# Attention inside a scan-paced kernel: one stream of 64 steps with the values product two steps behind the scores, and the branch announced earlier

## The chip, the cores and the metric

The kernel runs on one core of one Trainium2 chip. The metric is the time of one execution on the device, in microseconds (us); the time before is the median of three runs. Engines are called PE (TensorE, the matrix engine; PEld is its weight load), DVE (VectorE), ACT (ScalarE), POOL (GpSimd) and SP (SyncE, which issues nearly all DMAs). Each engine takes its instructions from a queue of its own, in the order in which the program was built.

## The reference, cut to what matters

Four images of 1024 tokens with 256 channels go through a layer with a convolution and a state-space scan (64 states), a grouped convolution, graph attention with a mixture of experts, and a second state-space layer (16 states) with another mixture of experts. The part that the change touches is the attention over 4096 tokens with 8 heads of 32 channels and a mask from an edge list:

```python
Q, K, V = (proj(Wq, bq), proj(Wk, bk), proj(Wv, bv))
scores = jnp.einsum('bhnd,bhmd->bhnm', Q, K) / jnp.sqrt(jnp.float32(hd))
mask = jnp.zeros((N, N), dtype=bool).at[edge_index[0], edge_index[1]].set(True)
scores = jnp.where(mask[None, None], scores, -jnp.inf)
attn = jax.nn.softmax(scores, axis=-1)
attended = jnp.einsum('bhnm,bhmd->bhnd', attn, V)
...
out = attended @ Wo + bo
y = x + out
```

A layer norm of `y` follows. The x that enters holds 4 images of 1024 tokens, each of which the kernel handles as a batch of its own with the same mask, so there are four attentions of 1024 x 1024 x 8.

## The kernel before, in words

**The scan sets the frame.** `scans` (L364) walks 1280 units. For unit k, SP loads `dA` (512 KB, replicated, `load`, four units ahead), ACT takes its exponential (`decay`, two units ahead), PE spreads the input into a two-bank PSUM tile `ps_rep` (`first`, one unit ahead, two buffers), DVE multiplies it by a row (1.2 us) and runs the scan (2.3 us), POOL multiplies the result by another row, and every second unit PE collects two results into `ps_y` (`pair`). The order of each engine's queue is written out by this loop.

**The stages ride along.** Everything else is a list of stages (`STAGES`), written as generators. Twice per unit the loop may run pieces of the current stage up to its next `yield` (`advance`, L538), at most `TICKS` = 2 pieces at a time and only while a table of assumed costs (`Metered.COST`) says that no engine is ahead of DVE's clock. The values that are yielded aren't used for that. So a `yield` is a place where scan instructions can slip in between. When a scan needs the output of a stage that isn't done, the rest of that stage is built with no scan beside it (`need`, L525; the flag `self.alone`). That happens in the fourth attention, from its 25th step of 64 on.

**Attention** (`attention`, L1174) projects queries, keys and values, bounds the scores (`large_scores`), adds two bias rows on POOL, and then calls `shift` (L1299) and `all_heads` (L1234).

- `shift`: where the bound is too large for a plain exponential, row maxima are computed and put into `mT`; with the given inputs the flag `large` is 0 and the work is skipped. Four engines (PE, DVE, ACT, SP) load the flag into a register and take a `tc.Switch` with two arms there and then. POOL takes no part.
- `heads` (L1377) handles one pair of heads against one half of the queries in eight steps, one per block of 128 keys. `scores(kb)` runs two f32 products of depth 32 into two PSUM tiles `ps_sc` (tag "s", two buffers in all), adds `mT` and the mask as bf16 products, and ACT writes the exponentials of both heads to `p` (three buffers). `values(kb)` multiplies `p` by the values and by ones (for the row sums), four f32 products into four column groups of the PSUM tile `acc` (one buffer). With a scan beside it the order is `pipe(scores, values, cut=True)`: values one step behind scores, and a `yield` after each. Alone, an empty step is put between them, so values are two steps behind, and the scores use the larger PSUM tiles of the scan (`ps_sx`) with one exponential of 128x1024.
- After eight steps the pipe runs empty, and ACT copies `acc` to `raw` and `sums`. After every second pair `divided` follows (a reciprocal on DVE, a product on POOL), interleaved with the next pair's steps.
- `projected` (L1435) multiplies half of the attended tokens by `Wo` into PSUM tiles that `ps` hands out in turn (tags "s", "s", "acc"); DVE adds. For the first half of the queries it stands between two head pairs of the second half, and `normed` is interleaved with the pair after that.

```python
        if alone:
            yield from self.pipe(range(TB), scores, lambda kb: None, values, cost=1.3)
        else:
            yield from self.pipe(range(TB), scores, values, cost=1.3, cut=True)
        nc.scalar.copy(raw[at : at + 64, c, :], acc[:64, :])
        nc.scalar.copy(sums[at : at + 64, c, :], acc[64:, :])
```

Of the kernel before, what the change touches and what calls it, by code (L numbers as in the profile page):

```python
# [7 lines left out]
F32 = mybir.dt.float32  # L8
# [8 lines left out]
P = 128  # L17
NB = 4
L = 1024
TB = L // P  # L20
C = 256
# [111 lines left out]
class Hybrid:  # L133
    def __init__(self, ctx, tc, a, out):
        self.ctx, self.tc, self.nc, self.a = ctx, tc, tc.nc, a
        self.out = out.rearrange("b h w c -> (b h w) c")
        nc = self.nc
        self.const = const = ctx.enter_context(tc.tile_pool(name="const", bufs=1))
        self.dram = ctx.enter_context(tc.tile_pool(name="dram", bufs=1, space=DRAM))

        self.ident = const.tile([P, P], F32, name="ident")
        make_identity(nc, self.ident)
        self.identb = const.tile([P, P], BF16, name="identb")
        nc.vector.tensor_copy(self.identb, self.ident)
# [12 lines left out]
        self.w_in0 = self.weight(const, "L0_conv_w_in", 2)  # L157
        for _ in self.norm(const, self.x0, TB, self.x0, "ln0"):
            pass

        self.blocks = const.tile([P, P], F32, name="blocks")
        make_block_diagonal(nc, self.blocks, 4)
        self.states = {0: 64, 3: 16}
        self.mem = {}


# [1007 lines left out]
    def attention(self, b, tb):  # L1174
        nc, tc, vec = self.nc, self.tc, self.vec
        with tc.tile_pool(name=f"at{b}", bufs=1, side="right") as op:
            xa = op.tile([P, TB, C], F32, name="xa")
# [8 lines left out]
            with tc.tile_pool(name=f"aa{b}", bufs=1, side="right") as fp:  # L1186
# [5 lines left out]
                def project(item):  # L1192
# [16 lines left out]
                    project, cost=1.7,  # L1209
# [14 lines left out]
                    nc.scalar.copy(v[:, 2 * j : 2 * j + 2, :], ps)  # L1224

                yield from self.pipe(range(TB // 2), values, cost=1.7)
            yield from self.add_rows(xa, self.bo, TB)
            yield from self.add_rows(tb, self.beta, TB)
            with tc.tile_pool(name=f"ab{b}", bufs=1, side="right") as fp:
                yield from self.shift(fp, qT, kT, mT, maskT, large)  # L1230
            with tc.tile_pool(name=f"ac{b}", bufs=1, side="right") as fp:
                yield from self.all_heads(fp, tb, qT, kT, v, maskT, mT, xa, wo)

    def all_heads(self, fp, tb, qT, kT, v, maskT, mT, xa, wo):  # L1234
        nc = self.nc

        def divided(raw, sums, c):
            nc.vector.reciprocal(sums[:, c, :], sums[:, c, :])
            yield 2.0
            nc.gpsimd.tensor_tensor(raw[:, c, :], raw[:, c, :], sums[:, c, :], ALU.mult)  # L1240
            yield 0.5

        then = iter(())
        for nh in range(2):
            raw, sums = (fp.tile([P, 2, 512], F32, tag=t, name=t, bufs=2) for t in ("raw", "sums"))
            for hp in range(4):
                for n, cost in enumerate(self.heads(fp, raw, sums, qT, kT, v, maskT, mT, nh, hp)):
# [12 lines left out]
            first = raw  # L1262
        yield from then
        y = yield from self.projected(fp, 1, raw, xa, wo)
        yield from self.normed(fp, tb, 1, y)

    def large_scores(self, fp, qT, kT, large):

# [27 lines left out]
        nc.vector.tensor_copy(large, most[:, 0:1])  # L1296
        yield 0.5

    def shift(self, fp, qT, kT, mT, maskT, large):  # L1299


        nc, tc = self.nc, self.tc
        E = mybir.EngineType
        go = {
            E.PE: nc.tensor, E.DVE: nc.vector, E.Activation: nc.scalar, E.SP: nc.sync,
        }
# [67 lines left out]

        yield from self.pipe([(c, g) for c in range(2) for g in range(2)], turn, cost=0.8)

    def heads(self, fp, raw, sums, qT, kT, v, maskT, mT, nh, hp):  # L1377

        nc = self.nc
        qs = slice(nh * 512, (nh + 1) * 512)
        c, at = hp // 2, 64 * (hp % 2)
        alone = self.alone
        acc = self.psum.tile([P, 512], F32, tag="acc", name="ps_at", bufs=1)
        got = {}

        def scores(kb):
# [11 lines left out]
            for i in range(2):  # L1401
# [4 lines left out]
            got[kb] = p = fp.tile([P, 2, 512], F32, tag="p", name="p", bufs=3)  # L1406
# [7 lines left out]
            for i in range(2):  # L1414
                nc.scalar.activation(p[:, i, :], two[i], AF.Exp)

        def values(kb):
            p = got.pop(kb)
            for i in range(4):
                h = 2 * hp + i % 2  # L1420
                nc.tensor.matmul(
                    acc[32 * i : 32 * i + 32, :],
                    lhsT=v[:, kb, h * HD : (h + 1) * HD] if i < 2 else self.ones,
                    rhs=p[:, i % 2, :],
                    start=(kb == 0), stop=(kb == TB - 1), tile_position=(0, 32 * i),
                )
# [490 lines left out]
```

## Time and profile before

| | |
|---|---|
| median of 3 runs | 6605.04 us (6598.39 to 6610.3) |
| the profiled execution: its time | 6610.56 us |
| the profiled execution: span, first to last instruction | 6608.8 us |
| mean granted PE clock | 0.834 |
| scan units | 1280: multiply 1213 ns, scan 2284 ns on DVE |
| attentions, first to last scores (us from the span's start) | 1420.7 to 1696.5, 2541.2 to 2817.4, 3954.0 to 4231.7, 5363.4 to 5584.6 |
| last scan-free stretch of attention 3 | from 5464.3 |
| an exponential, `p` | 595 ns (128x512), 1023 ns (128x1024) |
| a copy of `acc` (ACT) | 577 and 581 ns |
| `sums` reciprocal (DVE), `raw` product (POOL) | 3327 and 1266 ns |
| `y_at` add of a projection (DVE) | 692 ns |
| loads of the flag `large` on the sequencers of PE, DVE, ACT, SP | about 0.3 us each, at 1409.8 to 1413.5 in attention 0 |
| end of the write of `large` by DVE, attention 0 | 1388.9 |

All instructions that the planner counts are recorded in one helper, so nearly all have line L124 in the profile; they are told apart by the tiles that they write. "x<-y" means that tile x is written from y; an f32 product shows as two records. The name behind an idle time is what ended the wait; "issue" means that the engine waited for nothing that the profile shows. A busy PE isn't a PE at its peak, since the ends of its matmuls are modelled; the distance from one start to the next is the surer measure.

### The profile page before, as it was taken

What the parts mean: (1) busy time and instruction counts of PE and PEld (TensorE: products, weight loads), DVE (VectorE), ACT (ScalarE), POOL (GpSimd) and SP (SyncE); (2) the same over time, 40 slices, a digit from 0 to 9 for tenths busy, and PEclk for the clock granted to TensorE, in tenths of its full rate; (3) what the DMA queues carried; (4) which work ended last, traced back from release to release, by engine and by line L of the source; (5) the groups of instructions that cost most, each with busy time, mean ns of one, the idle gap of its engine ahead of it and who ended that gap; (6) DMA issues with size and microseconds to landing.
All of it is one profiled execution on the core that took longest, in us unless ns stands there. A gap on an engine that the chain in (4) does not pass through costs nothing. (4 is left out here: it accounts for less than half of the span.)

```text
span 6608.8 us, 59799 instructions
## 1 busy us (share of the span) xinstructions
PE 5331.1 (81%) x20236; PEld 2161.6 (33%) x20320; DVE 5140.0 (78%) x4310; ACT 3438.2 (52%) x4113; POOL 3642.9 (55%) x1793
## 2 busy tenths in 40 slices
PE   6667868679797568979689779898699688978979
PEld 2022312222342022234145232243255222524656
DVE  3978989988799997889889987898999971248411
ACT  3346566345477334557558445477487344245411
POOL 2857677755458665545856665556756651055200
PEclk8667868689798579979789789898699789877989
DMA  2454555643355566335645664345555750156221
GB/s 103 145 161 159 175 165 163 192 141 113 109 167 173 183 169 152 112 119 179 190 143 170 196 157 129 107 143 174 185 164 163 198 135 15 45 144 159 72 64 35
DMA packets 348113, 936.91 MB, mean 142 GB/s; under 512 B 37140, under 2 KB 119648, under 8 KB 346144
## 3 DMA queue, kind: packets, MB, share of 16 engines
q1 hardware_dynamic: 345616, 930.35, 46.3%
q0 software_dynamic: 2128, 2.13, 0.2%
q8 instruction: 172, 2.82, 0.2%
q14 instruction: 197, 1.61, 0.1%
HBM read 842.59 MB, written 93.95 MB: 142 GB/s over the span
## 5 line engine op out<-in xcount | busy, mean ns | idle before, releaser
L124 POOL TENSOR_TENSOR h<-h,rows 128x1024 f32<-128x1024 f32 x1280 | 3029.7, 2369 | 1948.9 <-DVE h L124 1736.3
L124 DVE TENSOR_TENSOR_SCAN h<-dA,ps_rep 128x1024 f32<-128x1024 f32 x1280 | 2923.9, 2284 | 169.3 <-issue 31.2
L124 DVE TENSOR_TENSOR ps_rep<-ps_rep,rows 128x1024 f32<-128x1024 f32 x1280 | 1552.8, 1213 | 254.0 <-PE ps_rep L124 253.7
L124 ACT ACTIVATE dA<-dA,A_L_conv_A_log 128x1024 f32<-128x1024 f32 x1024 | 1149.8, 1145 | 598.6 <-DMA dA<-dt 554.5
L124 PE MATMUL ps_rep<-S,spread_L_conv_A_log 96*128 96x512 bf16 x2048 | 762.1, 462 | 715.3 <-DVE h L124 694.5
L124 PE MATMUL ps_y<-h,collect_L_conv_A_log 128*32 128x512 f32 x4096 | 795.5, 759 | 70.4 <-POOL h L124 69.9
L124 PE MATMUL ps_h<-xTm,we 128*128 128x512 f32 x1536 | 717.2, 606 | 1.4 <-DVE tb L124 1.4
L124 PE MATMUL ps_e<-we,h_m 128*128 128x256 f32 x3072 | 699.3, 380 | 2.3 <-ACT h_m L124 2.3
L124 ACT ACT_TABLE_LOAD x501 | 642.8, 1283 | 52.0 <-PE ps_h L124 38.6
L124 PEld LDWEIGHTS <-spread_L_conv_A_log 96*128 96x128 bf16 x2048 | 160.7, 103 | 1489.7 <-DVE h L124 1195.1
L124 PEld LDWEIGHTS ps_e<-we,h_m 128*128 128x128 f32 x3072 | 579.9, 190 | 146.3 <-issue 45.5
L124 DVE SCALAR_TENSOR_TENSOR tb<-ps_e,cw,tb 128x256 f32<-128x256 f32 x512 | 220.7, 474 | 408.0 <-PE ps_e L124 407.6
L124 ACT ACTIVATE h_m<-ps_h,cols 128x512 f32<-128x512 f32 x384 | 260.4, 687 | 487.6 <-PE ps_h L124 484.8
L124 ACT ACTIVATE p<-ps_sc 128x512 f32<-128x512 f32 x432 | 234.4, 595 | 470.5 <-PE ps_sc L124 320.0
L124 PEld LDWEIGHTS ps_h<-xTm,we 128*128 128x128 f32 x1536 | 292.4, 194 | 338.5 <-issue 294.1
L124 ACT ACTIVATE dA<-dA,A_L_attn_A_log 128x1024 f32<-128x1024 f32 x256 | 290.5, 1146 | 199.5 <-DMA dA<-dt 164.8
L124 PE MATMUL ps_at<-p,v 128*32 128x512 f32 x1024 | 359.9, 610 | 37.8 <-ACT p L124 25.2
L124 PE MATMUL ps_rep<-S,spread_L_attn_A_log 96*128 96x512 bf16 x512 | 184.4, 448 | 177.0 <-DVE h L124 166.1
L124 PE MATMUL ps_sc<-qT,kT 32*128 32x512 f32 x864 | 249.3, 648 | 30.7 <-issue 22.9
L124 PE MATMUL ps_at<-p,ones 128*32 128x512 f32 x1024 | 271.9, 610 | 0.0
L124 PE MATMUL ps_cv<-pad,diag 128*128 128x512 f32 x576 | 262.0, 597 | 0.0
L124 PEld LDWEIGHTS ps_y<-h,collect_L_conv_A_log 128*32 128x32 f32 x4096 | 109.8, 119 | 458.5 <-issue 237.1
(327 smaller groups left out, 4916.1 us busy)
## 6 DMA issues: line engine op xcount, KB each, us to landing
dA<-dt SPq DMA_DIRECT2D x1280, 512.0 KB
we<-in_L_ffn_W_dram SPq DMA_DIRECT2D x64, 512.0 KB
parts<-parts SPq DMA_DIRECT2D x64, 384.0 KB
S<-parts SPq DMA_DIRECT2D x96, 256.0 KB
dt<-sp_r SPq DMA_DIRECT2D x64, 256.0 KB
y<-yo SPq DMA_DIRECT2D x128, 128.0 KB
y_back<-y SPq DMA_DIRECT2D x64, 256.0 KB
we<-in_L_ffn_w_dram SPq DMA_DIRECT2D x64, 256.0 KB
```

Source lines behind the costliest of these rows:

```text
L124: return got(*args, **kw)
```

## The change

`heads` no longer runs one head pair; it returns two functions, `scores(step)` and `values(step)`, that take a triple (query half, head pair, key block). `all_heads` walks all 64 triples in one loop: values of the step two before, a yield, scores of this step, a yield, then one piece of the work that waits in a list (`then`). Into that list go `divided` after every second pair and, after the first query half, `finished` (projection and norm of that half), which thus runs piece by piece between the steps of the second half and takes its PSUM tiles from tag "s". Whether a step runs alone is asked per step and no longer per pair; the lag is two in both cases. Both halves' `raw` and `sums` tiles are taken at the start.

The flag is loaded by the four engines right after the values projection (`nc.values_load`), some five scan units ahead of the branch, and `tc.mark_branch_hint_location` puts the branch hint there. The `Switch` becomes a `tc.If` on the loaded value.

```diff
+        E = mybir.EngineType
+        self.sides = (E.PE, E.DVE, E.Activation, E.SP)
...
                 yield from self.pipe(range(TB // 2), values, cost=1.7)
+            go = nc.values_load(large, engines=self.sides, min_val=0, max_val=1)
+            tc.mark_branch_hint_location(f"large{b}", go, engines=self.sides)
             yield from self.add_rows(xa, self.bo, TB)
             yield from self.add_rows(tb, self.beta, TB)
             with tc.tile_pool(name=f"ab{b}", bufs=1, side="right") as fp:
-                yield from self.shift(fp, qT, kT, mT, maskT, large)
+                yield from self.shift(fp, qT, kT, mT, maskT, go, f"large{b}")
...
-        then = iter(())
-        for nh in range(2):
-            raw, sums = (fp.tile([P, 2, 512], F32, tag=t, name=t, bufs=2) for t in ("raw", "sums"))
-            for hp in range(4):
-                for n, cost in enumerate(self.heads(fp, raw, sums, qT, kT, v, maskT, mT, nh, hp)):
-                    yield cost
-                    if n >= 3:
-                        more = next(then, None)
-                        if more is not None:
-                            yield more
-                yield from then
-                then = iter(())
-                if nh and hp == 0:
-                    y = yield from self.projected(fp, 0, first, xa, wo)
-                    then = self.normed(fp, tb, 0, y)
-                if hp % 2:
-                    then = divided(raw, sums, hp // 2)
-            first = raw
-        yield from then
-        y = yield from self.projected(fp, 1, raw, xa, wo)
-        yield from self.normed(fp, tb, 1, y)
+        then, steps = [], [(nh, hp, kb) for nh in range(2) for hp in range(4) for kb in range(TB)]
+        halves = [
+            [fp.tile([P, 2, 512], F32, tag=t, name=t, bufs=2) for t in ("raw", "sums")]
+            for _ in range(2)
+        ]
+        scores, values = self.heads(fp, halves, qT, kT, v, maskT, mT)
+        for n in range(len(steps) + 2):
+            if n >= 2:
+                values(steps[n - 2])
+                yield 1.3
+            if n < len(steps):
+                scores(steps[n])
+                yield 1.3
+            if then:
+                more = next(then[0], None)
+                if more is None:
+                    then.pop(0)
+                else:
+                    yield more
+            nh, hp, kb = steps[n - 2]
+            if n >= 2 and kb == TB - 1 and hp % 2:
+                then.append(divided(*halves[nh], hp // 2))
+                if nh == 0 and hp == 3:
+                    then.append(self.finished(fp, tb, 0, halves[0][0], xa, wo, "s"))
+        for more in then:
+            yield from more
+        yield from self.finished(fp, tb, 1, halves[1][0], xa, wo)
+
+    def finished(self, fp, tb, nh, att, xa, wo, tag=None):
+        y = yield from self.projected(fp, nh, att, xa, wo, tag)
+        yield from self.normed(fp, tb, nh, y)
...
-        go = {e: eng.value_load(large, min_val=0, max_val=1) for e, eng in go.items()}
         clock = dict(self.clock)
-        for arm in tc.Switch(go, 2):
-            if arm == 1:
-                for _ in self.row_max(fp, qT, kT, mT, maskT):
-                    pass
+        with tc.If(go, preferred_fallthrough_block=True, label=label):
+            for _ in self.row_max(fp, qT, kT, mT, maskT):
+                pass
...
-    def heads(self, fp, raw, sums, qT, kT, v, maskT, mT, nh, hp):
+    def heads(self, fp, halves, qT, kT, v, maskT, mT):
...
+            if kb == 0:
+                acc[0] = self.psum.tile([P, 512], F32, tag="acc", name="ps_at", bufs=1)
...
-        if alone:
-            yield from self.pipe(range(TB), scores, lambda kb: None, values, cost=1.3)
-        else:
-            yield from self.pipe(range(TB), scores, values, cost=1.3, cut=True)
-        nc.scalar.copy(raw[at : at + 64, c, :], acc[:64, :])
-        nc.scalar.copy(sums[at : at + 64, c, :], acc[64:, :])
-
-    def projected(self, fp, nh, att, xa, wo):
+            if kb == TB - 1:
+                raw, sums = halves[nh]
+                nc.scalar.copy(raw[at : at + 64, c, :], acc[0][:64, :])
+                nc.scalar.copy(sums[at : at + 64, c, :], acc[0][64:, :])
+
+        return scores, values
+
+    def projected(self, fp, nh, att, xa, wo, tag):
...
-            got[j] = ps = self.ps("ps_wo", (P, 2, C))
+            got[j] = ps = (
+                self.psum.tile([P, 2, C], F32, tag=tag, name="ps_wo", bufs=2) if tag
+                else self.ps("ps_wo", (P, 2, C))
+            )
```

More of the change, by code (lines that the diff above doesn't have):

```diff
@@ L1297, in large_scores, with shift @@
         yield 0.5
-    def shift(self, fp, qT, kT, mT, maskT, large):
+    def shift(self, fp, qT, kT, mT, maskT, go, label):
         nc, tc = self.nc, self.tc
[L1303 to L1306, printed above, removed]
-        go = {e: eng.value_load(large, min_val=0, max_val=1) for e, eng in go.items()}
         clock = dict(self.clock)
-        for arm in tc.Switch(go, 2):
-            if arm == 1:
-                for _ in self.row_max(fp, qT, kT, mT, maskT):
-                    pass
+        with tc.If(go, preferred_fallthrough_block=True, label=label):
+            for _ in self.row_max(fp, qT, kT, mT, maskT):
+                pass
         self.clock.update(clock)
@@ L1375, in row_max, with scores @@
         yield from self.pipe([(c, g) for c in range(2) for g in range(2)], turn, cost=0.8)
-    def heads(self, fp, raw, sums, qT, kT, v, maskT, mT, nh, hp):
+    def heads(self, fp, halves, qT, kT, v, maskT, mT):
         nc = self.nc
[L1383 to L1389, printed above, removed]
+        got, acc = {}, {}
+        def scores(step):
+            nh, hp, kb = step
+            qs = slice(nh * 512, (nh + 1) * 512)
+            c, at = hp // 2, 64 * (hp % 2)
+            alone = self.alone
             if alone:
@@ L1405, in scores @@
                 )
-            got[kb] = p = fp.tile([P, 2, 512], F32, tag="p", name="p", bufs=3)
+            got[step] = p = fp.tile([P, 2, 512], F32, tag="p", name="p", bufs=3)
             for i in range(2):
@@ L1415, in scores, with values @@
                 nc.scalar.activation(p[:, i, :], two[i], AF.Exp)
-        def values(kb):
-            p = got.pop(kb)
+        def values(step):
+            nh, hp, kb = step
+            c, at = hp // 2, 64 * (hp % 2)
+            if kb == 0:
+                acc[0] = self.psum.tile([P, 512], F32, tag="acc", name="ps_at", bufs=1)
+            p = got.pop(step)
             for i in range(4):
@@ L1421, in values @@
                 nc.tensor.matmul(
-                    acc[32 * i : 32 * i + 32, :],
+                    acc[0][32 * i : 32 * i + 32, :],
                     lhsT=v[:, kb, h * HD : (h + 1) * HD] if i < 2 else self.ones,
```

## Prediction

> **What bounds the kernel now.** I read the page's busy times first, then the tensor engine's waits in the first attention, the same stretches side by side, and the timeline of single steps. The page says that no engine bounds the whole:
>
> ```profile
> PE   5331.1 (81%) x20236; PEld 2161.6 (33%) x20320; DVE 5140.0 (78%) x4310; ACT 3438.2 (52%) x4113; POOL 3642.9 (55%) x1793
> ```
>
> DVE carries the 1280 scan units (1.21 us multiply plus 2.28 us scan, 3.5 us a unit) and all stages ride beside them, in queues of fixed order. So what counts is where DVE stands still. The table of stretches (the idle before attention 0, attentions 0 from first to last scores, the part of attention 3 that runs without scans):
>
> ```profile
> 1413.60:1420.70 7.10, 0.00 (x0) 0.00 (x0) 0.79 (x2) 0.00 (x0) 5.03 (x3) 0.50 0.31 85
> 1420.70:1696.50 275.80, 261.95 (x1358) 72.72 (x1380) 220.03 (x138) 140.67 (x206) 148.22 (x66) 0.99 0.34 115
> 5464.30:5584.60 120.30, 115.59 (x625) 29.51 (x632) 11.08 (x18) 49.11 (x56) 7.55 (x6) 0.96 0.00 1
> ```
>
> After the length come busy PE, PEld, DVE, ACT, POOL, then PE's clock. In the second line PE is busy 95% and DVE 80%: a scan unit takes 4.6 us here instead of 3.5. PE sets the pace in attention. The waits of that stretch say what it loses:
>
> ```profile
> PEld ps_at L124 <- ACT p L124: 58.6, 116, 1.0
> DVE ps_rep L124 <- PE ps_rep L124: 45.1, 41, 4.7
> DVE h L124 <- issue: 6.3, 1, 6.3
> ```
>
> PE's weight loads for the values product wait for the exponential 116 times; DVE waits 45.1 us for the scan's input product, which stands behind that in PE's queue. One step with its scan unit, from the timeline:
>
> ```profile
> 1691.78 1.13 PE L124 MATMUL ps_sc<-qT,kT 32*128 32x512 f32 x4
> ...
> 1693.50 0.60 PE L124 MATMUL ps_rep<-S,spread_L_conv_A_log 96*128 96x512 bf16 x2
> 1693.55 1.08 ACT L124 ACTIVATE p<-ps_sc 128x512 f32<-128x512 f32 x2 [1.77 <-PE ps_sc L124]
> ...
> 1694.19 0.14 PEld L124 LDWEIGHTS ps_at<-p,v 128*32 128x32 f32 x2 [0.59 <-ACT p L124]
> ...
> 1694.68 0.11 PEld L124 LDWEIGHTS ps_at<-p,v 128*32 128x32 f32 x1 [0.35 <-ACT p L124]
> ```
>
> The values product of a step starts when the first head's exponential is done and stops again, 0.5 us later, for the second's. Attention 3's last 40 steps already run two behind, and show a step without that wait:
>
> ```profile
> 5488.80 1.13 PE L124 MATMUL ps_sx<-qT,kT 32*128 32x512 f32 x4
> ...
> 5490.61 0.62 PE L124 MATMUL ps_at<-p,v 128*32 128x512 f32 x2
> ...
> 5491.60 1.13 PE L124 MATMUL ps_sx<-qT,kT 32*128 32x512 f32 x4
> ```
>
> Scores to values 1.81 us, values to scores 0.99: 2.81 a step, where the scan-free steps of attention 0 take 3.83. Last, the branch:
>
> ```profile
> 1412.56 1.03 PE L124 MATMUL ps_rep<-S,spread_L_conv_A_log 96*128 96x512 bf16 x2 [0.34 <-DVE h L124]
> ...
> 1419.94 2.29 DVE L124 TENSOR_TENSOR_SCAN h<-dA,ps_rep 128x1024 f32<-128x1024 f32 x1 [6.31 <-issue]
> ...
> 1420.74 1.32 PE L124 MATMUL ps_sc<-qT,kT 32*128 32x512 f32 x2 [7.15 <-issue]
> ```
>
> DVE and PE stand still together and wait for no engine.
>
> [...] It shows 0.50 before the first scores; the clock is full again from 1427.2 on, and the first step takes 6.77 us against 3.83. [...] So I take the cost of each piece from one start to the next[...].
>
> **The change, part by part.** Pieces on PE, start to next start where nothing waits, from the timeline of attention 0: scores (S) 1.72 to 1.81, say 1.77; values (V) 0.97; the scan's input product (R) 0.54; the scan's output product (Y) about 0.95 (V and Y together 1.90); half an output projection (W) 1.82.
>
> *The lag.* From first to last scores attention 0 has 63 S, 63 V, 58 R, 30 Y, 2 W: 111.5 + 61.1 + 31.3 + 28.5 + 3.6 = 236.0 of the measured 275.8. The missing 39.8 are the waits for p (about 1.1 us where nothing stands between S and V, 0.65 where R does) and some 3 of half clock. The changed program has, in PE's built order, 63 S, 62 V, 57 R, 29 Y, 2 W in the same place: 111.5 + 60.1 + 30.8 + 27.6 + 3.6 = 233.6. V now reads an exponential a whole step old. I add 2.9 for the half clock, which stays (it began at 1403.3, before the branch), and the new waits. (a) S must wait until the last exponential has left its two PSUM buffers: it ends 2.84 us after its S began, the next S follows at 2.77 or later, so only some 0.1 us where no R lies between; and ACT, with 141 of 276 us busy, has room for the decays queued before it. (b) At a head pair's end V waits for two copies of acc (0.58 each), which the S between hides. (c) The projection of the first half takes the scores' buffers: the next S waits until DVE has added the result. R, Y, V, R (3.0 us) stand between, DVE needs 4.8 (R 0.65, multiply and scan 3.5, add 0.69): 1.8, the second time about 2.1, together 3.9. Behind the waiting S stand all R's, so DVE waits with it. For (a) and (b) I take 2 us, between 0 and 5. So 242.4 and a gain of 33.4 us, three times: 100.2.
>
> Can DVE keep up? An R may start when the scan two before it is done, so DVE has about 3 us of slack (two R's 7.5 us apart against 0.65 + 3.5), and a reciprocal of 3.35 just fits. DVE's idle time from 1413.6 to 1706.5 is 292.9 - 226.8 = 66 us, more than I take. The input loads (dA) take 14 us from issue to use here and about 4 us where they are waited for, so a faster pace doesn't meet them.
>
> *Attention 3*, first to last scores 221.3 us, has 40 steps with the lag already. Pieces: 113.1 + 60.8 + 10.3 + 10.5 + 3.6 = 198.3, plus 2.9 clock and 4 for the norm's work on ACT that delays exponentials (now about 7 on four steps): 205.2. Gain 16.1: it comes from the 24 steps with scans, from head pairs that no longer drain, and from the projection that no longer stands alone.
>
> *The end of attention.* Now the last two V come together, so the last copies, reciprocal (3.35) and product (1.26), which the last projection waits for (W waits 5.0 us at 1706.5), start 1 us later: -1.2 each, -4.8.
>
> *The branch.* Each engine loads the flag some five scan units (18 us) earlier, behind a wait for DVE's write of it at 1388.9, which is long done; the load is 0.3 to 0.5 us on the sequencers and hidden by what their engines have queued. What stands behind it on each queue, SP's dA loads among them, have more than that in hand. [...] If it works, about 0.5 of 7.1 us remain: 6.6 times 4 = 26.4. If not, 0[...].
>
> *Elsewhere* the order shifts by one scan unit against the mixture of experts and what follows; 18 of 596 table loads fall away in the built order, on ACT, which isn't the bound: 0, between -20 and +20.
>
> Sum: 100.2 + 16.1 + 26.4 - 4.8 = 137.9. The profiled execution took 6610.6 (span 6608.8), 5.5 above the median of 6605.0: 6473 for it, 6467 for the median.
>
> **The rivals.** [...] it was in the kernel before too, 0.2 us ahead of the branch[...]. 6467 + 26 = 6493. *Half of the stream's gain is lost* because PE and DVE are both over 90% busy and only a unit apart, or ACT puts its decay before the exponential that S waits for (1.15 us a step): 6467 + 58 = 6525. For it: S, unlike V, now has two exponentials to wait for; against it: the 3 us of slack. *Slower:* the shift by a unit, after each attention, puts expert and projection matmuls against other scan units; outside attention some 1080 units take 4 to 4.4 us, not 3.5, because of just such places. If that costs over 0.13 us a unit (138 / 1080) the gain is gone, at 0.15 the time is 6625. Against it: nothing in those stages was edited, and the shift is one unit.
>
> **The numbers.** Forecast 0.58, hint dead 0.17, half the stream 0.18, slower 0.07. The forecast's low end leaves out (a), (b), (c), the half clock, the norm and the tail (39 us): 6428. To leave out no more than 2 in 10 the range reaches from 6425 to 6550, where both middle rivals hold together. A measurement of this kernel tells about 0.2% (13 us) from no change. Faster 0.90, same 0.03, slower 0.07.
>
> **What would show it.** Right: attention 0 from first to last scores near 242 us, steps at 2.8 without and about 3.7 on the mean with a scan unit; "PEld ps_at <- ACT p" almost gone; DVE's wait for ps_rep in that stretch down from 45 to about 15; no gap above 1 us before the first scores; two gaps of about 2 us at the first-half projection. Wrong: a new wait of ps_sc for ACT p on most steps, "issue" gaps of 6 us at the branch or elsewhere on PE, or stretches between attentions that differ by more than 10 us.

## The result, and the profile after

The changed kernel takes 6499.1 us (median of 4 runs, 6496.3 to 6504.5), the kernel before beside it 6607.7 (4 runs). The ratio is 0.9837, with a 95% interval from 0.9823 to 0.985: faster by 1.5 to 1.8%. Forecast were 6467 us and a gain of 138; the gain is 109 by the medians and 111.5 by the two profiled spans (6608.8 and 6497.3). The total is some 30 us off, and the parts are further off than the total.

The table of stretches, for the changed kernel: the end before attention 0, attentions 0, 1 and 2 from first to last scores, and the last 120 us of attention 3. After the length come busy PE, PEld, DVE, ACT, POOL, then PE's clock.

```profile
1407.20:1408.50 1.30, 1.00 (x3) 0.13 (x3) 1.06 (x2) 0.00 (x0) 1.30 (x2) 0.50 0.13 41
1408.50:1660.40 251.90, 241.01 (x1340) 64.22 (x1362) 215.01 (x135) 138.65 (x205) 148.86 (x68) 0.96 0.37 126
2498.80:2755.80 257.00, 244.92 (x1340) 64.37 (x1362) 213.05 (x135) 140.54 (x208) 146.85 (x67) 0.94 0.44 130
3885.50:4150.10 264.60, 250.80 (x1342) 65.08 (x1364) 212.49 (x134) 140.55 (x208) 146.11 (x66) 0.92 0.43 126
5362.40:5482.70 120.30, 118.72 (x679) 30.90 (x681) 14.53 (x20) 53.55 (x63) 11.87 (x8) 1.00 0.04 10
```

Attention 0 falls from 275.8 to 251.9 us. The three attentions with scans run the same program, and yet take 252, 257 and 265 us; the clock falls as they get longer (0.96, 0.94, 0.92). Something disturbs PE, and in each attention more often. The waits of attention 0, which answer to the prediction's:

```profile
DVE ps_rep L124 <- PE ps_rep L124: 22.3, 18, 4.2
DVE lny_w L124 <- ACT lny_r L124: 6.1, 1, 6.1
PEld ps_at L124 <- ACT p L124: 0.3, 1, 0.3
PEld ps_sc L124 <- ACT p L124: 23.1, 28, 0.8
```

The wait for p in front of the values product has gone from 58.6 us in 116 places to one of 0.3. The last line is the wait that the prediction named as a sign of being wrong, `ps_sc` for ACT's exponential (28 times, and 23 times more for a decay of ACT's); it costs nothing on ordinary steps, where scores to scores is the bare sum of the pieces, as the next lines show. DVE's wait for its input product has halved (45.1 to 22.3, forecast about 15), and a wait inside a normalisation, 1.9 us before, has grown to 6.1. A step with its scan unit is as forecast:

```profile
1649.84 1.13 PE L124 MATMUL ps_sc<-qT,kT 32*128 32x512 f32 x4
...
1651.56 0.60 PE L124 MATMUL ps_rep<-S,spread_L_conv_A_log 96*128 96x512 bf16 x2
1651.60 1.09 ACT L124 ACTIVATE p<-ps_sc 128x512 f32<-128x512 f32 x2 [1.98 <-PE ps_sc L124]
...
1652.09 0.62 PE L124 MATMUL ps_at<-p,v 128*32 128x512 f32 x2
...
1653.08 1.13 PE L124 MATMUL ps_sc<-qT,kT 32*128 32x512 f32 x4
```

Scores to scores is 3.24 us, where it was 3.89; the values product starts while ACT still writes this step's exponential, because it reads one that is two steps old. The pieces are 1.72 for the scores, 0.53 for the scan's input product and 0.99 for the values. And the branch of attention 0:

```profile
1407.15 1.03 PE L124 MATMUL ps_rep<-S,spread_L_conv_A_log 96*128 96x512 bf16 x2 [0.34 <-DVE h L124]
...
1408.46 2.29 DVE L124 TENSOR_TENSOR_SCAN h<-dA,ps_rep 128x1024 f32<-128x1024 f32 x1 [0.24 <-DVEq L1318]
1408.48 2.17 PE L124 MATMUL ps_sc<-qT,kT 32*128 32x512 f32 x4 [0.30 <-PEq L1318]
```

PE's stop before the first scores is 0.30 us where it was 7.15, and DVE's is 0.24 where it was 6.31. At the other three branches PE still waits 2.26, 2.98 and 2.85 us (before: 7.96, 7.72, 7.82).

**Where the gain came from** (spans, us):

| part | forecast | measured |
|---|---|---|
| attentions 0 to 2, first to last scores | 3 x 33.4 = 100.2 | 23.9 + 19.2 + 13.0 = 56.1 |
| attention 3, first to last scores | 16.1 | 16.4 |
| PE's gaps at the four branches | 26.4 | 30.7 - 8.4 = 22.3 |
| end of attention and all else | -4.8 | 16.7 |
| sum | 137.9 | 111.5 |

**The two places where the stream loses.** The first half's projection, steps 37 to 39 of attention 0, from the timeline:

```profile
1548.44 1.99 PE L124 MATMUL ps_wo<-w_L_attn_Wo,raw 128*128 128x256 f32 x8 [0.53 <-ACT p L124]
...
1550.90 1.23 DVE L124 TENSOR_TENSOR ps_rep<-ps_rep,rows 128x1024 f32<-128x1024 f32 x1 [2.40 <-PE ps_rep L124]
...
1553.19 1.12 PE L124 MATMUL ps_sc<-qT,kT 32*128 32x512 f32 x2
1554.47 0.67 DVE L124 TENSOR_TENSOR y_at<-ps_wo,xa 128x512 f32<-128x512 f32 x1
...
1555.28 0.66 PE L124 MATMUL ps_sc<-qT,kT 32*128 32x512 f32 x1 [0.97 <-DVE y_at L124]
...
1557.66 3.50 PE L124 MATMUL ps_wo<-w_L_attn_Wo,raw 128*128 128x256 f32 x8 [0.53 <-ACT p L124]
...
1562.85 1.23 DVE L124 TENSOR_TENSOR ps_rep<-ps_rep,rows 128x1024 f32<-128x1024 f32 x1 [4.16 <-PE ps_rep L124]
```

Scores start at 1553.19 and their second half only at 1555.28, when DVE has added and freed the buffer. While they wait, the projection's second part, the values product and the scan's next input product stand behind them; PE's clock halves from 1558.0 for 3.4 us, and that part takes 3.50 us instead of 1.82. The three steps take 7.25, 9.56 and 6.38 us. Their pieces, at the prediction's prices, are three S (5.3), three V (2.9), four R (2.2), two Y (1.9) and two W (3.6): 15.9. The loss is 7.3 us; in attentions 1 and 2 (7.25, 10.75, 9.56) it is 11.7. It goes with the clock: in attentions 1 and 2 the clock is at half here twice, for 6.8 us each. In attentions 0 to 2 of this kernel and of the four below that leave the lag and this projection as they are (x1, x4, x7, x8), the three steps take 22.8 to 23.5 us where the clock was at half for 3.4 us, 26.4 where it was for 10.2, and 27.6 where it was for 13.7; which of the two leads isn't shown.

The other place is the first half's normalisation, steps 45 and 46:

```profile
1587.48 1.28 ACT L259 ACT_TABLE_LOAD   x1
1588.78 0.20 ACT L124 ACTIVATE lny_r<-lny_v 128x4 f32<-128x4 f32 x1
...
1589.25 0.16 DVE L124 TENSOR_TENSOR lny_w<-lny_r 128x4 f32<-128x4 f32 x1 [6.08 <-ACT lny_r L124]
...
1592.26 1.04 PE L124 MATMUL ps_rep<-S,spread_L_conv_A_log 96*128 96x512 bf16 x2 [3.56 <-DVE lny_b L124]
```

Read it backwards: PE waits for DVE to free a `ps_rep` buffer, DVE stands in front of a scan at a 0.16 us operation on four columns, and that waits for ACT's logarithm, which is queued behind a step's exponentials (1.08 us), a decay (1.15) and a table load (1.28). Two steps take 8.28 and 7.63 us where their neighbours take 3.35 and 4.20; the clock is at half for 10.2 us.

Attention 2 has a third place, steps 17 and 18 (7.93 and 7.94 us; 3.35 and 4.34 in attention 0):

```profile
3954.97 1.15 ACT L124 ACTIVATE dA<-dA,A_L_attn_A_log 128x1024 f32<-128x1024 f32 x1 [4.32 <-DMA dA<-dt]
...
3957.37 0.93 PE L124 MATMUL ps_at<-p,v 128*32 128x512 f32 x2 [3.35 <-ACT sums L124]
```

A scan's `dA` lands late, ACT waits 4.32 us for it, and the copies of `acc` (0.58 us each) stand behind it in ACT's queue, so that PE waits 3.35 us before the next head pair's values.

### The profile page after: what moved, and what is told of

It is laid out like the page before. It is cut to its first block, busy times and chain, and to the rows that moved or that the text cites. A ratio compares the mean times of both kernels' runs of the same rounds, so it can differ in the third digit from the quotient of the medians.

```text
span 6497.3 us, 59722 instructions
## 1 busy us (share of the span) xinstructions
PE 5253.9 (81%) x20235; PEld 2124.1 (33%) x20320; DVE 5119.6 (79%) x4310; ACT 3415.4 (53%) x4095; POOL 3646.8 (56%) x1793
## 5 line engine op out<-in xcount | busy, mean ns | idle before, releaser
L124 PE MATMUL ps_y<-h,collect_L_conv_A_log 128*32 128x512 f32 x4096 | 775.8, 767 | 61.5 <-POOL h L124 61.0
L124 PE MATMUL ps_at<-p,v 128*32 128x512 f32 x1024 | 277.6, 623 | 4.8 <-ACT sums L124 4.6
L124 PE MATMUL ps_sc<-qT,kT 32*128 32x512 f32 x864 | 262.9, 665 | 14.2 <-ACTq L1318 8.1
```

Source lines behind the costliest of these rows:

```text
L124: return got(*args, **kw)
```

## The experiments

My theory after the result: the lag does what the model says on every ordinary step, and the missing 44 us of the stream are these three places, each a wait in a fixed queue. The rival: the loss lies all over the stream, because PE and DVE stand only a unit apart, and the three places only show it. For each kernel the median is given, and its ratio to the kernel before with the 95% interval.

**x1: the announcement ahead of the branch, the flag loaded early.**

```diff
-            tc.mark_branch_hint_location(f"large{b}", go, engines=self.sides)
...
+        tc.mark_branch_hint_location(label, go, engines=self.sides)
         with tc.If(go, preferred_fallthrough_block=True, label=label):
```

> The changed kernel with one difference: the flag is loaded as early as before, but the branch is announced directly ahead of it instead of five scan units earlier. Theory [...]: PE and DVE stand 6 to 8 us without a wait ahead of each attention again, about 21 us in all (6.9 at the first branch, 4.5 to 4.8 at the others): 6499 + 21 = 6520. Rival (loading the flag early and the fall-through form of the branch do it, not the announcement): 6499.

6506.1 us, 0.9845 (0.9828 to 0.9861), as the rival said, but it decides nothing: the records show the announcement still right behind the load of the flag (which ends at 1396.36 on DVE; the announcement is at 1396.43) and 19 us ahead of the branch (1415.22). So it is the load, and not the mark in the source, that places the announcement. The program is instruction for instruction the changed kernel's, so this is a second measurement of it. As such it helps: its first scores come at 1416.9 instead of 1408.5, and its stretches between the attentions and behind the last differ from the changed kernel's by +2.4, -4.7, +1.1 and +3.3 us, and its four attentions by +4.2, -1.3, -4.8 and 0.0. So much varies with no change at all. In the order of the table above (without its sum), its gain splits into 57.9, 16.4, 19.7 and 8.8 us.

**x8: flag and announcement directly ahead of the branch.**

```diff
-            go = nc.values_load(large, engines=self.sides, min_val=0, max_val=1)
-            tc.mark_branch_hint_location(f"large{b}", go, engines=self.sides)
...
+        go = nc.values_load(large, engines=self.sides, min_val=0, max_val=1)
+        tc.mark_branch_hint_location(label, go, engines=self.sides)
```

> The changed kernel with the flag loaded, and the branch with it announced, directly ahead of the branch on every engine instead of five scan units earlier. The order of everything else is the same. Theory (the announcement needs the time of five units[...]): PE and DVE stand 6 to 8 us at each branch again, 6499 + 21 = 6520, between 6515 and 6527. Rival (the fall-through form of the branch, one compare instead of two[...]): below 6507, gaps of 1 to 3 us.

6514.5 us, 0.9862 (0.9847 to 0.9877): 15 us above the changed kernel by the medians, with intervals that overlap at their ends, and 8 above x1; but each of its four runs (6511.4 to 6523.2) is above all eight of those two. The trace says it more sharply. Attention 1's branch in this kernel:

```profile
2504.82 2.29 DVE L124 TENSOR_TENSOR_SCAN h<-dA,ps_rep 128x1024 f32<-128x1024 f32 x1 [0.45 <-DVEq L1318]
...
2510.82 2.17 PE L124 MATMUL ps_sc<-qT,kT 32*128 32x512 f32 x4 [6.48 <-DVE h L124]
```

PE's gaps are 5.18, 6.48, 6.22 and 6.28 us, 24.2 in all against 8.4 with the early load, a difference of 15.8. DVE, which stood 6 to 8 us in the kernel before, stands 0.45. Where PE stops is on record: the branch instruction of its sequencer (shown with the weight loads, PEldq) is what takes long, first in the changed kernel, then in x8 (four branches, shortest, median and longest in ns):

```profile
L1318 PEldq COMPARE_BRANCH  x4: 361/377/393, 1407.1 to 5274.0; - x4
L1318 PEldq COMPARE_BRANCH  x4: 4569/5830/5987, 1413.2 to 5286.7; - x4
```

In the kernel before it takes 5.53 to 6.54 us. So theory and rival each hold for one engine. PE's stop is its own branch, which takes 0.38 us (median) with the load and its announcement early and 5.83 with both late. DVE's stop is gone without the early announcement. In the kernel before it lies behind the second of two compares (which ends at 1414.54; the scan starts at 1419.94), and the fall-through form has one; that fits the form of the branch as the cause, but no run changes the form alone, so this is argued and not shown.

**x2: the branch alone, on the kernel before.** Its edit is the branch's part of the diff: `go` and the announcement behind the values projection, and `tc.If` in `shift`.

> The kernel before with the changed kernel's branch alone (flag loaded and announced at the end of the values projection, fall-through form); the heads are as before. Theory (the branch's gain is its own): 6607 - 21 = 6586, between 6580 and 6590, first-to-last scores of the attentions unchanged at 276, 276, 278 and 221 us. Rival (it pays only with the stream, or is lost where the work goes on): 6605.

6586.3 us, 0.997 (0.996 to 0.9979), between 14 and 26 us; the attentions stay at 276, 277, 279 and 218 us. The branch is worth about 20 us by itself.

**x3: one step behind instead of two.**

```diff
-        for n in range(len(steps) + 2):
-            if n >= 2:
-                values(steps[n - 2])
+        for n in range(len(steps) + 1):
+            if n >= 1:
+                values(steps[n - 1])
```

(with the two other places where `n - 2` stands)

> The changed kernel with the values product one step behind the scores instead of two; still one stream without a drain at the head pairs, branch announced early. Theory (the second step of lag is the gain, since values no longer wait for the exponential): scan-free steps go from 2.81 back to about 3.8 us, attentions 0 to 2 lose most of their 19 us each, attention 3 goes from 205 to about 245: 6499 + 57 + 40 = 6596, between 6570 and 6610. Rival (what pays is that head pairs no longer drain, seven times per attention): about 6510.

6677.8 us, 1.0104 (1.0079 to 1.0128): slower than the kernel before. Attentions 0 to 2 are back at 278, 276 and 275 us, so the whole gain there goes with the second step of lag; that the head pairs no longer drain doesn't show in the sum (this kernel, too, has the projection in its stream). Attention 3 takes 322 us where 245 were expected; the section on the hardware shows where most of that lies.

**x5: the first half's projection and normalisation behind the stream.**

```diff
                 then.append(divided(*halves[nh], hp // 2))
-                if nh == 0 and hp == 3:
-                    then.append(self.finished(fp, tb, 0, halves[0][0], xa, wo, "s"))
...
-        yield from self.finished(fp, tb, 1, halves[1][0], xa, wo)
+        for nh in range(2):
+            yield from self.finished(fp, tb, nh, halves[nh][0], xa, wo)
```

> The changed kernel with the first half's projection and normalisation taken out of the stream and put behind its end, ahead of the second half's. Theory (the stream lost its forecast gain at two places: about 9 to 13 us per attention where the projection holds the scores' buffers, about 8 us where DVE stands in the first half's normalisation behind ACT's logarithm): attentions 0 to 2 fall from 252, 257, 265 to about 235, 237, 245 us from first to last scores; at the end 3.6 us of projections and a few of the normalisation come in again, partly inside the 5.1 us that the last projection waits for its product; net some 12 to 15 us per attention with scans: 6455 to 6465. Rival (the loss is spread over the stream, because PE and DVE stand only a unit apart, and the two places only show it): 6495 to 6505, and attentions still near 250 us.

6493.2 us, 0.9833 (0.9814 to 0.9852): not to be told from the changed kernel. But the attentions are at 234.8, 236.3, 239.1 and 198.6 us, as the theory had it, with as many scan units in them as before (57 decays in each of the first three), and the rival is out: with the projection and its normalisation gone, the stream runs at the model's pace. What was gained inside (17, 21, 26 and 6 us) was given back behind: the stretches up to the next attention are longer by 15, 14 and 17 us, the last by 9. Part of it was made by this kernel itself; DVE behind its attention 0:

```profile
1680.38 0.69 DVE L124 TENSOR_TENSOR y_at<-ps_wo,xa 128x512 f32<-128x512 f32 x1 [5.27 <-POOL tb L124]
```

The second half's add waits for a tile that POOL still reads for the first half.

**x9: both projections, then both normalisations, behind the stream**, with the results in the freed tiles of the sums.

```diff
-        y = fp.tile([P, 4, C], F32, tag="y", name="y_at")
+        y = sums.rearrange("p a (b c) -> p (a b) c", c=C)
...
+        y = []
+        for nh in range(2):
+            y.append((yield from self.projected(fp, nh, *halves[nh], xa, wo)))
+        for nh in range(2):
+            yield from self.normed(fp, tb, nh, y[nh])
```

> Both halves' projections stand together behind the stream, the first filling the wait of the second for its product, and then both normalisations; the projections' results go into the freed tiles of the sums, so that the second add no longer waits for the first half's last sum on POOL (5.3 us in the trace of the kernel with the projection at the end). Theory (what that kernel gained in the stream, 17 to 26 us per attention, was given back behind it by this one wait and the chain of two normalisations, 15 us): attentions stay at 235, 237, 240 and 199 us, behind each attention some 8 us of the 15 come back: 6493 - 4 x 8 = 6461. Rival (work of projection and normalisation costs DVE and the chain the same wherever it stands): 6490.

6480.0 us, 0.981 (0.9796 to 0.9823). The stretches behind the attentions are still longer than the changed kernel's, by 12, 8, 9.5 and 8 us: some 5 us less than with x5 on the mean, and some 9 us of work that costs its time there too. Theory and rival are both half right.

**x4: the normalisation's vector operations two pieces later.**

```diff
         nc.scalar.activation(r, r, AF.Exp, scale=-0.5)
+        yield from [0.5] * late
...
-        yield from self.norm(fp, y, 4, y, "lny")
+        yield from self.norm(fp, y, 4, y, "lny", 0 if nh else 2)
```

(`late` is handed through `norm` to `rstd`, which becomes a generator)

> The changed kernel; the first half's normalisation waits two pieces between ACT's logarithm and exponential and the vector operations that read them, so that DVE no longer meets them in its queue before ACT has done them. Theory (DVE's 6.1 us wait for the logarithm, in front of a scan, costs two steps about 8 us in each attention with scans): attentions 0 to 2 some 8 us shorter (244, 249, 257), 6499 - 24 = 6475. Rival (PE's clock and its queue set these steps anyway, the wait only moves): attentions unchanged, 6495 to 6505.

6488.6 us, 0.9822 (0.9807 to 0.9838). Steps 45 and 46 take 3.24 and 4.38 us in all three attentions, instead of 15.9, 16.0 and 14.4 for the pair: 8.3, 8.4 and 6.8 us gone, as the theory had it. DVE now meets the logarithm when it is done:

```profile
1594.27 0.20 ACT L124 ACTIVATE lny_r<-lny_v 128x4 f32<-128x4 f32 x1
...
1595.00 0.14 DVE L124 TENSOR_TENSOR lny_w<-lny_r 128x4 f32<-128x4 f32 x1
```

Of these 24 us only about 10 are in the total. The attentions are at 248.0, 244.8 and 249.7 us, but between them this kernel is 7, 5 and 5 us longer and behind the last one 5, which the second measurement (x1) covers in part only. ACT has 18 instructions more, all of them table loads (596 for 578); x11 below has the same split without them and gives nothing back between the attentions. Whether they are the reason stays open.

**x6: the add at once behind the projection.**

```diff
+        if tag:
+            for j in range(2):
+                project(j)
+                add(j)
+                yield 1.7
+        else:
+            yield from self.pipe(range(2), project, add, cost=1.7)
```

> The changed kernel; the first half's projection hands its result to DVE at once, so that the add stands in DVE's queue ahead of the next scan units: right behind the scan of unit 329 instead of behind that of unit 331, in the first attention. Theory (steps 37 to 39 take 23 to 28 us instead of 11 plus 3.6 for the projection itself because the scores wait for a buffer that an add frees, and the add stands behind two whole scan units): the three steps fall to about 17 or 18 us, attentions 0 to 2 by 5 to 9 us each, and as in the kernel with the split normalisation about half of it is kept: 6499 - 12 = 6487. Rival (DVE then stands in the add until the projection is done, which costs the scans as much): 6499.

6476.1 us, 0.9793 (0.9775 to 0.9812), better than expected, though its five runs lie far apart (6457 to 6488). Steps 37 to 39 take 6.71, 6.20 and 4.24 us in each attention: 17.15 where they took 23.2, 27.6 and 27.6. DVE does stand at the add (5.5 us, from an early place in its queue), but PE gets on meanwhile, and its clock stays full through these steps: a step's four score products take 1.13 to 1.21 us in attention 0, where at half clock they take 2.08 (changed kernel, at 3960.07).

**x7: dA five units ahead.**

```diff
-            a = mp.tile([P, L], F32, tag="dA", name="dA", bufs=5)
+            a = mp.tile([P, L], F32, tag="dA", name="dA", bufs=6)
...
-            load(k + 4)
+            for m in range(loaded + 1, k + 6):
+                if m < k + 5 or m < len(units) and ("parts", *units[m][0], units[m][1]) in self.ready:
+                    load(m)
+                    loaded = m
```

(and one buffer for `yo` instead of two, for the space)

> The changed kernel with the scan's input dA loaded five units ahead instead of four (six buffers instead of five; the copy of the scan's result has one buffer instead of two to make room). Theory (in attention 2 one dA arrives 4.3 us late, and with ACT's queue behind it two steps lose 8 us; attention 1 loses some 1.5): attention 2 goes from 265 to about 257, 6499 - 10 = 6489, and more if ACT's waits for dA outside attention (2 to 5 us ahead of each branch) count. Rival (the loads share the same DMA engines, the one that is late is late whenever it is asked for): 6499.

6488.1 us, 0.9825 (0.9812 to 0.9839). Attention 2 takes 252.0 us, its steps 17 and 18 are 3.34 and 4.34; 8 of the 11 us. This is no chance of one execution: these two steps take 12.9 to 15.9 us together in all seven traces of the stream with two steps of lag and loads four units ahead, and 7.7 in the three with loads five ahead (x7, x10, x11). PE's gaps at the branches 1 to 3 fall from 2.26, 2.98 and 2.85 us to 0.30, 1.26 and 0.30: there ACT came late to its own branch, behind a `dA` it waited for (4.87 us and, for the next, 1.11 at branch 1 of the changed kernel), and the profile puts PE's wait down to ACT's branch (2.26 us there).

**x12: the same edit on the kernel before.**

> The kernel before, with dA loaded five units ahead in six buffers (and one buffer for the copy of the scan's result), nothing else. It asks whether the 11 us that the same edit gained on the changed kernel belong to the changed kernel's faster stream. Theory (they do: in the attentions of the kernel before no dA is waited for but one, while the changed kernel waits for several): within attention nothing changes, outside ACT waits for some fewer loads that others hide; 6606 - 3 = 6603, at most 6 us less. Rival (the late loads cost the same outside attention in both kernels): 6595, and the dA part of the loss has nothing to do with the change.

6604.4 us, 0.9998 (0.999 to 1.0007): nothing. The late loads are a cost of the faster stream.

**x10 and x11: all together, in two ways.** x10 is x9 with x7's loads (and both `yo` buffers); x11 leaves the projection in the stream and joins x4, x6 and x7.

> Both halves' projections and normalisations behind the stream, as in the kernel with both at the end, and dA loaded five units ahead in six buffers (the freed tile makes the room; the scan's result keeps its two). Theory (the two causes are independent: 19 us and 11 us below the changed kernel when taken alone): attentions at 235, 235, 235 and 199 us, PE's gaps at the branches under 1.5 us, 6480 - 11 = 6469. Rival (both remove the same late loads, in that the loads are late where the stream goes at full pace): 6480.

> The projection stays in the stream, with its three troubles treated one by one: the add at once behind the projection, the normalisation's vector operations two pieces behind ACT's, dA loaded five units ahead (one buffer for the copy of the scan's result). Theory (the troubles add up): attentions 0 to 2 at about 238 to 240 us including the first half's projection, 6499 - 11 - 11 - 12 = 6465. Rival (what is gained in the stream is mostly given back behind it, since a unit of the scan that no longer fits in the attention has to be done elsewhere at 4.2 us): 6480.

x10: 6468.0 us, 0.9784 (0.977 to 0.9797), as expected. x11: 6444.4 us, 0.9753 (0.974 to 0.9766), better than expected and the best here, 55 us below the changed kernel and 162 below the one before. Its attentions 0 to 2:

```profile
1416.30:1656.50 240.20, 234.46 (x1342) 62.34 (x1364) 215.09 (x135) 138.82 (x205) 148.92 (x68) 0.98 0.42 132
2492.00:2731.80 239.80, 233.71 (x1342) 62.38 (x1364) 214.50 (x135) 140.68 (x208) 148.29 (x68) 0.99 0.48 141
3857.30:4095.70 238.40, 232.64 (x1342) 62.15 (x1364) 214.61 (x135) 140.63 (x208) 148.47 (x68) 0.99 0.50 142
```

The three are nearly equal now, DVE's work in each is about what it was (215 us), and between them nothing is given back. Against x10, which has the same early loads, the first half's projection and normalisation cost 5 to 7 us inside the stream (x10's attentions 0 to 2 take 233 each), and 5 to 14 us in each stretch behind it.

## Why the prediction was right and where it was not

- **The lag on ordinary steps: right.** 2.81 us without a scan unit; 3.24 and 4.10 in turn with one, 3.67 on the mean against "about 3.7". The model's 242.4 without its own term for (c) and its two projections is 242.4 - 3.9 - 3.6 = 234.9; x5, which has neither in the stream, took 234.8 in attention 0. x10, in which no load is late either, took 232.8 to 233.0 in all three: 2 us less, the size of the terms (a) and (b), of which no step shows anything.
- **Attention 3: right**, 204.8 against 205.2, but in part by luck. In its scan-free part the scores don't take the buffers that the projection holds, and no decay stands in ACT's queue. No step shows the 4 us for the norm (steps 37 and 38 take 4.53 each, a step and half a projection, all later ones 2.81); instead the first two steps, at half clock, took 11.3 us, 2.2 more than in attention 0.
- **Term (c), the projection that holds the scores' buffers: the right place, the wrong size.** Forecast 3.9 us each, measured 7.3, 11.7 and 11.7: 19 us too little in all. The forecast counted PE's wait for the add (2 x 2 us, which is what the trace has: scores take 3.9 instead of 1.8) but not what comes with it in the trace: the next part waits 0.53 us for the delayed exponential, the clock is at half (for 3.4 us in attention 0, for 13.7 in the two others), DVE gets its input 2.4 and 4.2 us late and so adds late again. x6 took 6 to 10 us of it away by the add's place in the queue alone.
- **"DVE has about 3 us of slack": the step that failed.** It looked at multiply, scan and reciprocal and left out the first half's normalisation, though the list of pieces that the change interleaves holds it. In the kernel before DVE waited 1.9 us there, and no step showed it; with the faster stream it cost 8.3, 8.4 and 6.8 us. x4 shows it alone.
- **"A faster pace doesn't meet the dA loads": wrong in attention 2**, by 8.2 us. The 14 us were the time from issue to use at the old pace, and not what a load needs; in the faster stream about 11 are left. The load of steps 17 and 18 was issued at 3940.03 and used at 3954.97, after 14.9 us of which ACT waited 4.3, and exponentials and copies queue behind it on ACT. x7 and x12 show it.
- These account for the stream. Attention 0: 33.4 - 3.4 - 8.3 = 21.7, measured 23.9. Attention 1: 33.4 - 7.8 - 8.4 = 17.2, measured 19.2. Attention 2: 33.4 - 7.8 - 6.8 - 8.2 = 10.6, measured 13.0. The remaining 2 each have the size of (a) and (b).
- **The branch: right in kind, 22 instead of 26**, since at three branches ACT arrives late behind a `dA` and PE waits 2.26 to 2.98 us for it (x7). That the announcement, given early, takes the stop away was the author's estimate. It fits x8 on PE: same form, load and announcement late, and the branch instruction takes 4.6 to 6.0 us again; in the changed kernel it takes 0.36 to 0.39 us on PE and 0.07 to 0.09 on DVE. What PE waits for in the stop isn't shown. The profile has two DMA queues that it marks "instruction"; they carry 9 packets (0.09 MB) from 1414.3 to 1421.0, around the stop in the kernel before, and 2 from 1407.0 to 1408.5, around the changed kernel's branch, but no record ties PE's stop to them. On DVE it is not the announcement; by x8 it may be the form of the branch, which the prediction had not told apart.
- **The end of attention: as forecast in three of four.** The part of the last projection that waits for the product starts 11.05 us after the last scores instead of 9.97 in attentions 0 to 2, 1.1 later (forecast 1.2). In attention 3 nothing moves (10.14 in both): its last steps had the lag already, and the forecast counted it all the same.
- **All else: 16.7 us where -4.8 was said**, 21 apart, just over the bound of 20. 5.4 lie ahead of the first attention's branch and 9.6 behind the last scores; the second measurement of the same program (x1) moves these by 8.4 and 3.3 us and has 8.8 in place of the 16.7, so no cause can be named. They hide part of the stream's miss in the total, and that is luck.
- **The rivals.** "Half of the stream's gain lost" named 6525 and a loss on every step; the loss had nearly this size (44 us against 58 for half), but sat in two to three places, and the cause it names did not occur: ordinary steps take no more than the sum of their pieces. That x11 came to 6444 shows that nothing in the pace itself stood in the way. The rival at 6493, in which nothing is gained at the branches, is out by PE's gaps (30.7 us before, 8.4 after) and by x2. (The 6625 of the slower rival is 6629 by its own sum, 6467 + 1080 x 0.15.)

## What to carry to other kernels

When a stream of work gets faster, price again each irregular thing that rides in its queues (a projection, a small normalisation, a late load): a wait that had slack before can stop two engines now, and cost more than the wait that the profile names (a wait of 6.1 us cost up to 8.4 here, one of 4.3 cost 8.2, and PE's two of 1.0 for the add cost 7.3 to 11.7 together). In a queue of fixed order, look at where an operation stands that frees a buffer (x6 gained by putting it right behind its producer) and one that reads another engine's result (x4 gained in its steps by putting it two pieces later); both are moves of a line or two. And an experiment that takes the disturbance out altogether (x5) tells whether the model of the regular part holds, before one cures the places one by one.

## What the runs showed of the hardware that was not expected

**The same step ran at a granted clock of 1.00 for 34 us and at 0.50 for 151 us.** In x3's attention 3 PE waits 1.17 us in each scan-free step for an exponential. The stretches from 5438.5 on, cut where the clock changes (length, busy PE, PEld, DVE, ACT, POOL, clock):

```profile
5438.50:5472.60 34.10, 23.23 (x132) 5.41 (x136) 3.35 (x1) 10.37 (x11) 1.26 (x1) 1.00 0.00 0
5472.60:5486.30 13.70, 12.19 (x37) 3.93 (x39) 0.00 (x0) 2.05 (x2) 0.00 (x0) 0.50 0.00 0
5486.30:5499.90 13.60, 11.10 (x63) 4.06 (x66) 3.55 (x11) 3.07 (x3) 0.00 (x0) 1.00 0.01 1
5499.90:5650.80 150.90, 122.43 (x373) 22.69 (x370) 4.17 (x6) 30.69 (x36) 6.28 (x5) 0.50 0.00 0
```

The first ten scan-free steps take 4.05 us each with the clock full, and PE is busy 68% of the first stretch. At 5472.6 the clock falls, in a step with no other wait than these; the projection begins only at 5484.2. The next steps take 4.89 and 6.51 us. During the projection's products the clock comes back. At 5499.9 it falls again, once more without a new kind of wait, and from then on a step takes 6.5 us, to the end, though PE is busy 81% of the time and does the same work:

```profile
5603.38 1.07 PE L124 MATMUL ps_at<-p,v 128*32 128x512 f32 x2 [1.17 <-ACT p L124]
...
5609.89 1.07 PE L124 MATMUL ps_at<-p,v 128*32 128x512 f32 x2 [1.17 <-ACT p L124]
```

Between two waits PE works for 5.3 us, as far as the profile shows, and the clock stayed at half for 151 us. It fell after waits of 1.17 us in x3, and in the changed kernel at 1558.0, in the projection, after waits of 0.97 and 0.53; at the normalisation it fell at 1592.1, at the end of a wait of 3.56. What decides it isn't shown here, and since the ends of matmuls are modelled, the 5.3 us may hide stops that the record lacks.

The half clock makes most of attention 3's 322 us: 23 steps at 6.5 us instead of 4.05 are 56 of the 77 us above the expected 245. In the changed kernel the clock is at half just where the stalls cost more than their waits: in attention 0 for 3.4 us at the projection and for 10.2 at the normalisation. In x11's attentions 0 to 2, with 0.98, 0.99 and 0.99 on the mean, it isn't at half once it has come back at their start.
